# A four-layer convolution kernel: fourth neighbour and softplus sums to TensorE, a fifth scan product to VectorE

## The chip, the core and the metric

The kernel runs on one core of one Trainium2 chip. The metric is the device time of the whole kernel in microseconds. Work is spread over TensorE (PE; its weight loads are shown as PEld), VectorE (DVE), ScalarE (ACT) and GpSimd (POOL). SyncE (SP) issues most DMAs; POOL issues the indirect ones. Each engine takes its instructions in the order of the program and stops at an instruction whose inputs are not ready.

## The reference

Four layers are applied to an image batch x of shape (4, 128, 128, 128), each as x + layer(groupnorm(x)), all in f32.

- Layer 0 is a deformable 3x3 convolution. A small convolution gives, for each pixel and each of the 9 taps, an offset and a mask. Each tap is sampled bilinearly from four neighbours, each with its own weight:

```
corner(y0i, x0i, (1 - ly) * (1 - lx)) + corner(y0i, x0i + 1, (1 - ly) * lx)
  + corner(y0i + 1, x0i, ly * (1 - lx)) + corner(y0i + 1, x0i + 1, ly * lx)
```

  The sample, times its mask, is projected by a 128x128 matrix per tap and summed over the taps.
- Layer 1 is a dilated 5x7 convolution to 16 channels, followed by two small projections.
- Layer 2 norms the image, splits its channels, and passes one half through a selective scan in four directions with 16 states: h = h * exp(delta * A) + (delta * u) * B, and y = sum over the states of h * C. Here delta = softplus(dt), and B and C come from projections of u.
- Layer 3 is a 3x3 convolution with a term that subtracts neighbouring sums.

## The kernel before

**Two strands.** The scan of layer 2 is the main strand. It visits 4 images x 4 directions x 32 blocks of 512 positions, 512 blocks in all. Everything else is the side strand: generators that issue a few instructions each time they are pulled. `together` issues one scan slot (16 a block), then pulls the side until its share of progress matches. While image b is scanned, the side finishes image b-1 (after the scan, then layer 3) and prepares image b+1 (layer 0, layer 1, and the part of layer 2 ahead of the scan). So layer 0 runs once alone, for the first image, and three times beside the scan. `keep_order` fixes each engine's order as written. `loads` sets `beside["busy"]` to "POOL" while layer 0 runs beside the scan, and to "PE" for other side stages; the scan reads it to choose engines.

**Layer 0.** One sample is one tap of one block of 4 rows of 128 pixels: 32 x 9 = 288 samples an image. `weave` runs a software pipeline over samples with these steps:

1. `gather` (L416): four indirect DMAs by POOL fetch, for 128 pixels each, the four neighbours of 128 channels, into a tile g of [128, 4 rows, 4 neighbours, 128]. There are four such tiles.
2. `weigh_low` (L431), two steps later: ACT multiplies neighbours 1 and 2 in place by their per-pixel weights, and neighbour 0 into a PSUM bank, pw. There is one such bank.
3. `weigh` (L445): DVE adds neighbours 1 and 2 to pw in two additions (L450), then forms v = g3 * weight + pw for each row (L453). v has two tiles.
4. `turn` (L457), one step later: PE transposes the four 128x128 pieces of v into one PSUM bank, pst (L461).
5. `copy` (L463) moves pst to SBUF by ACT; `project` (L467) multiplies it by the tap's weights, accumulating over nine taps; `add` adds the residual at the ninth.

`order` (L504) fixes the order within a step: weigh_low of neighbour 1 and turn; then add, gather and weigh_low of neighbour 2; then weigh_low of neighbour 0; then copy and the work on the next strip's offsets; then weigh and project.

**The scan.** A block has four groups g of four states sets ng. For each group, DVE forms h = du * B (L972, 128x2048), with du in the one PSUM bank named dub, refilled by ACT in `inputs_up` (L876). For each ng, ACT makes the decay exp (L899) and DVE runs the scan (L1018). `outputs` (L935) multiplies half a group of h, 128x1024, by C: eight such products a block. PE sums them (L913, `sums`). `carry_on` saves the last column of h on ACT before the product overwrites h. While `beside["busy"]` is "POOL", the second half of every group is multiplied on DVE and the first half on POOL, so four of eight each; otherwise all are on POOL.

**prepare** (L822) makes delta two blocks ahead, one step a slot. PE multiplies u to pdt (in the dub bank). ACT takes e = |pdt|, delta = relu(pdt), then e = exp(-e), one_e = 1 + e, ln = log(one_e), one_e = one_e - 1. POOL then does delta = delta + (ln + (e - one_e)) in three additions (L858, L860, L862), one a slot, and du = delta * u (L864). The correction e - one_e restores what the rounding of 1 + e lost. The block's delta and du are stored to DRAM and read back spread over partitions.

Of the kernel before, what the change touches and what calls it, by code (L numbers as in the profile page):

```python
# [10 lines left out]
F32 = mybir.dt.float32  # L11
# [7 lines left out]
P = 128  # L19
# [4 lines left out]
N = R * W  # L24
# [7 lines left out]
NG = 4  # L32
# [79 lines left out]
def conv_preact_kernel(ctx: ExitStack, tc: tile.TileContext, a: dict, nb: int):  # L112
    nc = tc.nc
    x_in, out = a["x"], a["out"]

    const = ctx.enter_context(tc.tile_pool(name="const", bufs=1))
    small = ctx.enter_context(tc.tile_pool(name="small", bufs=2))
    dram = ctx.enter_context(tc.tile_pool(name="dram", bufs=2, space=DRAM))
    pss = ctx.enter_context(tc.tile_pool(name="scps", bufs=1, space=PSUM))
# [11 lines left out]
    beside = {}  # L131
# [19 lines left out]

    ident = const.tile([P, P], F32, name="ident")
    make_identity(nc, ident)
    started = len(tc.nc.cur_bb.bb.instructions)
    nc.scalar.preload_act_table_set(LOG_EXP)
    gmat = load(const, a["gmat"], [P, P], "gmat_sb")
# [23 lines left out]
    with ExitStack() as s:  # L180
# [3 lines left out]
        for k in range(NDIR):  # L184
            pw = bank(0, "pwd")
# [112 lines left out]
    def layer0(st):  # L298
# [5 lines left out]
        with ExitStack() as s:  # L304
# [30 lines left out]
            got = {}  # L335
# [108 lines left out]

            def weigh(n):  # L445
                i, k, j, q = where(n)
                wv, g = got["i", j][0], got.pop(("g", n))
                pw = got.pop(("w", n)).rearrange("p (r c) -> p r c", r=R)
                for c in (1, 2):
                    nc.vector.tensor_add(pw, pw, g[:, :, c, :])  # L450
                got["v", n] = v = gp.tile([P, R, P], F32, name="v", bufs=2)
                for r in range(R):
                    nc.vector.scalar_tensor_tensor(  # L453
                        v[:, r, :], g[:, r, 3, :], wv[:, r, q, k, 3:4], pw[:, r, :], ALU.mult, ALU.add
                    )

            def turn(n):  # L457
                v = got.pop(("v", n))
                got["t", n] = pst = bank(1, "pst")
                for r in range(R):  # L460
                    nc.tensor.transpose(pst[:, r * P : (r + 1) * P], v[:, r, :], ident)  # L461

            def copy(n):  # L463
                got["c", n] = smp = pp.tile([P, N], F32, name="smp")
# [322 lines left out]
    def scan(pull):  # L787
# [4 lines left out]
        seq = []  # L792
# [26 lines left out]
                    flush()  # L819
                blocks[t]["u"] = load(sp, blk(us[k % 2], i), [P, N], "u", bufs=2)  # L820

        def prepare(t):  # L822

            st, k, i, back = seq[t]
            c = blocks[t]
            if (st["b"], k) not in carries:
                carries[st["b"], k] = carry = small.tile([P, NST], F32, name="carry")
                nc.vector.memset(carry, 0.0)
            c["carry"] = carries[st["b"], k]
            u = c["u"]  # L830
            pdt = pss.tile([P, N], F32, name="pdt", tag="dub")
            nc.tensor.matmul(pdt, wd[:, k, :], u, start=True, stop=True)  # L832
            yield

# [12 lines left out]
            px = pss.tile([P, N], F32, name="pxbc", tag="dub")  # L847
            nc.tensor.matmul(px, xbc[:, k, :], u, start=True, stop=True)  # L848
            ln = sp.tile([P, N], F32, name="ln", bufs=1)
            nc.scalar.activation(ln, one_e, AF.Ln)  # L850
            yield
            nc.scalar.activation(one_e, one_e, AF.Identity, bias=minus)  # L852
            bc = sp.tile([2 * NST, N], F32, name="bc")
            nc.scalar.copy(bc, px[0 : 2 * NST])  # L854
            c["bc"] = bcd = dram.tile([2, NST, N], F32, name="bcd", bufs=4)
            store(bcd.rearrange("j s t -> (j s) t"), bc)
            yield
            nc.gpsimd.tensor_sub(e, e, one_e)  # L858
            yield
            nc.gpsimd.tensor_add(ln, ln, e)  # L860
            yield
            nc.gpsimd.tensor_add(delta, delta, ln)  # L862
            yield
            nc.gpsimd.tensor_mul(du, delta, u)  # L864
            c["steps"] = sd = dram.tile([P, 2 * N], F32, name="stepsd", bufs=4)
            store(sd, steps.rearrange("p j t -> p (j t)"))
# [93 lines left out]
        for t, (st, k, i, back) in enumerate(seq):  # L960
            c = blocks[t]
            carry = c["carry"]
            more = prepare(t + 2) if t + 2 < len(seq) else iter(())
            if t > 0:
                fetch(t + 3)
            for g in range(NG):
                then = (t, g + 1) if g + 1 < NG else (t + 1, 0)
# [7 lines left out]
                on_vector = beside.get("busy") == "POOL"  # L975
# [13 lines left out]
                for ng in range(NG):  # L989
                    n = g * NG + ng  # L990
                    if ng == 1:
                        decays(at + 1)
                        if before[0] >= 0 and not on_vector:
                            outputs(*before, 1)
                        if g > 1 and then[0] < len(seq):
                            inputs_up(*then)
                        if earlier[0] >= 0:
                            sums(*earlier, 1)
                    if ng == 2 and g == 1 and t > 0:
                        finish(t - 1)  # L1000
                    if n % NST and ng != 2:
                        next(more, None)
                    if ng == 2 and before[0] >= 0 and on_vector:
                        outputs(*before, 1, nc.vector)
                    if ng == 2:
                        carry_on(t, g, 0)
                        decays(at + 2)
                        next(more, None)
                        if g < 2:
                            inputs_up(*then)  # L1010
                    if ng == 3:
                        outputs(t, g, 0)
                        if before[0] >= 0:
                            sums(*before, 0)
                    o, f = h[:, ng, :], c["a", n]
                    if back:
                        o, f = o[:, ::-1], f[:, ::-1]
                    nc.vector.tensor_tensor_scan(o, f, o, carry[:, n : n + 1], ALU.mult, ALU.add)  # L1018
                    if ng == 3:
                        decays(at + 3)  # L1020
                    yield (t * NST + n + 1) / slots
            for _ in more:
                pass
        t = len(seq) - 1
# [408 lines left out]
```

## Time and profile before

| what | value |
|---|---|
| median of the timed runs | 22396.11 us (22355.13 to 22411.09, 3 runs) |
| the profiled execution: its own time, its span | 21942.39 us, 21940.6 us |
| busy over the span: PE, DVE, ACT, POOL | 74%, 86%, 75%, 78% |
| samples of layer 0 alone, beside the scan | 288, 864 |
| L424 gathers (POOL) | 4608, mean 988 ns |
| L450 additions (DVE) | 2304, mean 693 ns |
| L461 transposes (PE records) | 4608, mean 371 ns |
| L939 products: on POOL; on DVE | 3740, mean 2363 ns; 356, mean 1323 ns |
| L858, L860, L862 softplus additions (POOL) | 512 each, means 1272, 1274, 1291 ns |

Busy time is the union of an engine's instructions. For PE, one f32 matmul leaves two records; the ends of records are modelled, so distances between starts are the safer measure of cost. A row of a timeline merges equal instructions: start in us, length in us, engine, line, operation, output and inputs, shapes and count. A row of waits names who waited, for whom, the total us, the number of times and the longest. The span counts from the first instruction; the timed runs are of executions without a profile.

### The profile page before, as it was taken

How to read it: one execution, taken by the hardware profiler on the slowest of the kernel's cores; microseconds unless marked ns; L12 is line 12 of the kernel's file. 1: busy time of each engine (PE TensorE's matmuls, PEld its weight loads, DVE VectorE, ACT ScalarE, POOL GpSimd, SP SyncE). 2: the span in 40 equal slices, each digit the busy share in tenths (PEclk: the TensorE clock that was granted, in tenths of full speed). 3: DMA queues.
4: the chain of work that ended last, by engine and by line, in shares of the span. 5: the costliest groups of instructions: out<-in, count | busy, mean ns of one | idle time of the engine just before them, and what ended most of it. 6: DMA issues, size and time to landing. Idle time of an engine off the chain costs nothing. (4 is left out here: it accounts for less than half of the span.)

```text
span 21940.6 us, 177438 instructions
## 1 busy us (share of the span) xinstructions
PE 16289.2 (74%) x37000; PEld 6635.1 (30%) x37000; DVE 18903.6 (86%) x19821; ACT 16411.9 (75%) x37350; POOL 17213.1 (78%) x11496
## 2 busy tenths in 40 slices
PE   4557866666788878666688888766687878778788
PEld 1223322222333333222233333322233323233333
DVE  4554899999998899899998899998998899999994
ACT  5885868888688766788868776688877877666673
POOL 4773878877888888778788888787878889877884
PEclk6668988888999989888899999887898999999999
DMA  8775687777766968777776787777776677555674
GB/s 250 229 226 178 210 287 243 243 237 237 235 215 216 256 224 272 233 250 249 241 231 220 221 254 249 245 246 245 246 256 210 219 217 233 194 195 202 208 233 132
DMA packets 2578828, 5038.92 MB, mean 230 GB/s; under 512 B 1060736, under 2 KB 1333576, under 8 KB 2435408
## 3 DMA queue, kind: packets, MB, share of 16 engines
q1 hardware_dynamic: 2209104, 3819.31, 53.3%
q0 software_dynamic: 368640, 1208.25, 18.1%
q14 instruction: 782, 6.41, 0.1%
q8 instruction: 302, 4.95, 0.1%
HBM read 4082.03 MB, written 874.52 MB: 226 GB/s over the span
## 5 line engine op out<-in xcount | busy, mean ns | idle before, releaser
L1018 DVE TENSOR_TENSOR_SCAN h<-pa,carry,h 128x512 f32<-128x512 f32 x8192 | 9998.0, 1267 | 495.7 <-ACT pa L899 283.6
L913 PE MATMUL yacc<-h,gather_sb 128*128 128x512 f32 x15264 | 8338.4, 676 | 1770.5 <-POOL h L939 1170.3
L939 POOL TENSOR_TENSOR h<-h,cb 128x1024 f32<-128x1024 f32 x3740 | 8787.1, 2363 | 1093.0 <-ACT carry L933 1076.8
L424 POOL DMA_INDIRECT g<-table,idx x4608 | 4552.7, 988 | 1616.0 <-issue 1059.3
L899 ACT ACTIVATE pa<-spread,neg_a 128x512 f32<-128x512 f32 x8192 | 5488.2, 682 | 271.7 <-DVE h L1018 270.8
L972 DVE TENSOR_TENSOR h<-dub,bb 128x2048 f32<-128x2048 f32 x2048 | 4659.9, 2275 | 418.9 <-ACT dub L879 162.9
L913 PEld LDWEIGHTS yacc<-h,gather_sb 128*128 128x128 f32 x15264 | 3133.5, 216 | 6082.3 <-issue 3392.2
L461 PE MATMUL pst<-ident,v 128*128 128x128 f32 x4608 | 1194.5, 371 | 2578.5 <-DVE v L453 2236.1
L438 ACT ACTIVATE g<-g,wt 128x128 f32<-128x128 f32 x9216 | 2877.5, 389 | 301.5 <-DMA g<-table,idx 298.5
L933 ACT COPY carry<-h 128x2 f32<-128x2 f32 x4096 | 769.0, 188 | 3035.9 <-DVE h L1018 3031.8
L450 DVE TENSOR_TENSOR pw<-pw,g 128x512 f32<-128x512 f32 x2304 | 1597.7, 693 | 1073.6 <-ACT pw L438 1022.6
L438 ACT ACTIVATE pw<-g,wt 128x128 f32<-128x128 f32 x4608 | 1693.6, 368 | 291.2 <-DVE v L453 177.4
L461 PEld LDWEIGHTS pst<-ident,v 128*128 128x128 f32 x4608 | 718.5, 158 | 3938.6 <-issue 1901.5
L858 POOL TENSOR_TENSOR e<-e,one_e 128x512 f32<-128x512 f32 x512 | 651.2, 1272 | 1294.8 <-ACT one_e L852 1258.2
L471 PE MATMUL acc<-smp,w_sb 128*128 128x512 f32 x2304 | 1550.9, 762 | 56.1 <-DVE x L478 52.8
L879 ACT COPY dub<-spread 128x512 f32<-128x512 f32 x2048 | 1198.7, 585 | 391.2 <-DVE h L972 212.7
L453 DVE SCALAR_TENSOR_TENSOR v<-g,wt,pw 128x128 f32<-128x128 f32 x4608 | 1292.8, 342 | 113.7 <-DVE pw L450 2.8
L1238 PE MATMUL p<-xn,w_l_sb 128*128 128x508 f32 (+2 forms) x2304 | 1132.9, 610 | 1.8 <-ACT xn L1217 1.8
L848 PE MATMUL pxbc<-u,xbc_sb 128*128 128x512 f32 x1024 | 590.5, 660 | 394.4 <-DVE h L972 385.9
L721 PE MATMUL px<-win,convw_sb 128*128 128x508 f32 (+1 forms) x1536 | 786.8, 610 | 36.1 <-DMA win<-win 34.8
L941 POOL TENSOR_TENSOR h<-h 128x512 f32<-128x512 f32 x558 | 710.8, 1274 | 43.7
L832 PE MATMUL pdt<-u,wd 128*128 128x512 f32 x1024 | 562.4, 632 | 193.3 <-DVE h L972 127.4
(170 smaller groups left out, 16751.3 us busy)
## 6 DMA issues: line engine op xcount, KB each, us to landing
spread<-stepsd SPq DMA_DIRECT2D x2048, 512.0 KB, 4.3
bb<-bcd SPq DMA_DIRECT2D x512, 1024.0 KB, 8.0
cb<-bcd SPq DMA_DIRECT2D x512, 1024.0 KB, 9.1
stepsd<-steps SPq DMA_DIRECT2D x512, 512.0 KB, 3.5
table<-gt SPq DMA_DIRECT2D x512, 256.0 KB, 4.8
g<-table,idx POOLq DMA_INDIRECT x4608, 3.8
u<-urow SPq DMA_DIRECT2D x256, 256.0 KB, 3.5
yrow<-y SPq DMA_DIRECT2D x256, 256.0 KB, 9.3
```

The source lines that it names most:

```text
L424: nc.gpsimd.indirect_dma_start(out=g[:, r].rearrange("p q c -> p (q c)"), out_offset=None, in_=table, in_offset=bass.IndirectOffsetOnAxis( ...
L438: nc.scalar.activation(pw[:, r * P : (r + 1) * P] if c == 0 else g[:, r, c, :], g[:, r, c, :], AF.Copy, scale=wv[:, r, q, k, c : c + 1],)
L450: nc.vector.tensor_add(pw, pw, g[:, :, c, :])
L453: nc.vector.scalar_tensor_tensor(v[:, r, :], g[:, r, 3, :], wv[:, r, q, k, 3:4], pw[:, r, :], ALU.mult, ALU.add)
L461: nc.tensor.transpose(pst[:, r * P : (r + 1) * P], v[:, r, :], ident)
L471: nc.tensor.matmul(got["a", i], w0[:, k, :], got.pop(("c", n)), start=k == 0, stop=k == KK - 1)
L879: nc.scalar.copy(p, blocks[t]["p", g][:, 1, :])
L899: nc.scalar.activation(pa, blocks[t]["p", g][:, 0, :], AF.Exp, scale=neg_a[:, k, n : n + 1])
L913: nc.tensor.matmul(c["y"], gather[:, g, :], c["h", g][:, ng, :], start=g == 0 and ng == 0, stop=last and ng == parts[-1] and not second,)
L939: engine.tensor_mul(h, h, c["cb"][:, 2 * half : 2 * half + 2, :])
L972: nc.vector.tensor_tensor(h, c["pdu", g].unsqueeze(1).to_broadcast([P, NG, N]), c["bb"], ALU.mult)
L1018: nc.vector.tensor_tensor_scan(o, f, o, carry[:, n : n + 1], ALU.mult, ALU.add)
```

## The change

Three things change, the last two only while layer 0 runs beside the scan.

- `weigh` adds neighbour 1 alone. The addition of neighbour 2 moves to PE: for each of the four rows, `turn` now issues two matmuls with the identity as moving operand into the same piece of pst, one of g's neighbour 2 and one of v, accumulated. They are ordinary f32 matmuls where a transpose was. The tile g is thus read last by PE in `turn`, not by DVE in `weigh`. This holds for all 1152 samples.
- `prepare` with `on_pe` replaces POOL's three softplus additions by four accumulating matmuls, e, -one_e, ln and delta, with the identity or a negated identity `less` as weights, into the bank dub; ACT copies the sum to delta a slot later. The step product du moves one slot later. To keep the bank's users in order, `inputs_up` of groups 2 and 3 moves from slot ng = 1 to ng = 2.
- The first half of the last group, too, is multiplied on DVE: five of eight products.

```diff
             def weigh(n):
                 i, k, j, q = where(n)
-                wv, g = got["i", j][0], got.pop(("g", n))
+                wv, g = got["i", j][0], got["g", n]
                 pw = got.pop(("w", n)).rearrange("p (r c) -> p r c", r=R)
-                for c in (1, 2):
-                    nc.vector.tensor_add(pw, pw, g[:, :, c, :])
+                nc.vector.tensor_add(pw, pw, g[:, :, 1, :])
...
             def turn(n):
-                v = got.pop(("v", n))
+
+                v, g = got.pop(("v", n)), got.pop(("g", n))
                 got["t", n] = pst = bank(1, "pst")
                 for r in range(R):
-                    nc.tensor.transpose(pst[:, r * P : (r + 1) * P], v[:, r, :], ident)
+                    dst = pst[:, r * P : (r + 1) * P]
+                    nc.tensor.matmul(dst, g[:, r, 2, :], ident, start=True, stop=False)
+                    nc.tensor.matmul(dst, v[:, r, :], ident, start=False, stop=True)
...
+            if on_pe:
+                yield
+                yield
+                pd = pss.tile([P, N], F32, name="psum", tag="dub")
+                for n, (t, sign) in enumerate(((e, ident), (one_e, less), (ln, ident), (delta, ident))):
+                    nc.tensor.matmul(pd, sign, t, start=n == 0, stop=n == 3)
+                yield
+                nc.scalar.copy(delta, pd)
+                yield
+            else:
+                nc.gpsimd.tensor_sub(e, e, one_e)
+                yield
+                nc.gpsimd.tensor_add(ln, ln, e)
+                yield
+                nc.gpsimd.tensor_add(delta, delta, ln)
+                yield
             nc.gpsimd.tensor_mul(du, delta, u)
...
-            more = prepare(t + 2) if t + 2 < len(seq) else iter(())
+            on_pe = beside.get("busy") == "POOL"
+            more = prepare(t + 2, on_pe) if t + 2 < len(seq) else iter(())
...
-                        if g > 1 and then[0] < len(seq):
+                        if g > 1 and then[0] < len(seq) and not on_pe:
                             inputs_up(*then)
...
-                        if g < 2:
+                        if (g < 2 or on_pe) and then[0] < len(seq):
                             inputs_up(*then)
                     if ng == 3:
-                        outputs(t, g, 0)
+                        outputs(t, g, 0, nc.vector if on_vector and g == NG - 1 else nc.gpsimd)
```

More of the change, by code (lines that the diff above doesn't have):

```diff
@@ L153, in conv_preact_kernel @@
     make_identity(nc, ident)
+    less = const.tile([P, P], F32, name="less")
+    nc.vector.tensor_scalar_mul(less, ident, -1.0)
     started = len(tc.nc.cur_bb.bb.instructions)
@@ L820, in fetch, with prepare @@
                 blocks[t]["u"] = load(sp, blk(us[k % 2], i), [P, N], "u", bufs=2)
-        def prepare(t):
+        def prepare(t, on_pe=False):
             st, k, i, back = seq[t]
@@ L857, in prepare @@
             yield
[L858 to L863, printed above, removed]
+            if on_pe:
[14 more added lines that the diff above has]
+                yield
             nc.gpsimd.tensor_mul(du, delta, u)
```

## The prediction

> **What bounds the kernel now.** I began with the busy shares by stretch of time, taken for the four stretches in which the deformable layer runs: once alone, then three times beside the scan. Columns: stretch and its length, then for each engine busy us and instructions, then the granted PE clock, DMA share and GB/s.
>
> ```profile
> 217.00:1665.00 1448.00, 837.37 (x2252) 315.83 (x2252) 828.07 (x2015) 1246.23 (x3754) 1091.82 (x1152) 0.66 0.76 226
> 3245.00:5330.00 2085.00, 1360.58 (x3440) 555.55 (x3438) 1925.04 (x2811) 1803.08 (x4930) 1658.89 (x1416) 0.83 0.74 241
> 8885.00:10840.00 1955.00, 1285.87 (x3286) 535.04 (x3287) 1760.32 (x2700) 1719.27 (x4762) 1556.34 (x1375) 0.80 0.76 245
> 14125.00:16060.00 1935.00, 1264.73 (x3242) 524.75 (x3242) 1740.73 (x2676) 1707.45 (x4736) 1549.83 (x1370) 0.80 0.76 246
> ```
>
> The engine columns are PE, PEld, DVE, ACT, POOL. Beside the scan (5975 us in all, 864 of the layer's 1152 samples) DVE looks busiest with 5426 us (91%), ACT has 5229 (88%), POOL 4765 (80%), PE 3911 (65%). The share of POOL misleads, as the timeline shows:
>
> ```profile
> 1005.58 0.95 POOL L424 DMA_INDIRECT g<-table,idx  x1 [0.30 <-issue]
> 1006.83 0.94 POOL L424 DMA_INDIRECT g<-table,idx  x1 [0.30 <-issue]
> 1008.08 0.94 POOL L424 DMA_INDIRECT g<-table,idx  x1 [0.30 <-issue]
> ```
>
> Gathers follow each other at 1.25 us, of which 0.30 counts as idle that nothing releases. A sample's four gathers hold POOL for 5.0 us. Alone, 288 samples x 5.03 is the whole 1448 us: POOL is full there. In the stretch from 8885 (27.9 blocks of the scan), POOL holds 1152 x 1.25 = 1440, 111 products x 2.37 = 263, softplus and step products 28 x 5.4 = 151: 1854 of the 1910 us from first to last gather, 97%. So POOL and DVE both lead, with ACT close behind. The waits of the stretch from 8840 say how DVE and ACT are tied:
>
> ```profile
> DVE pw L450 <- ACT pw L438: 134.2, 96, 5.1
> ACT pw L438 <- DVE v L453: 66.7, 64, 2.8
> ```
>
> The weighed sum has one PSUM bank; ACT refills it only when DVE has read it. ACT's waits in the three stretches sum to 655 us: DVE accounts for about 437 (scan 235, weighed sum 177, carry 26), landings of gathers for 110, PE for most of the rest.
>
> **PE's price list.** Ends are modelled, so I use starts.
>
> ```profile
> 9617.71 0.60 PE L461 MATMUL pst<-ident,v 128*128 128x128 f32 x4
> 9618.24 1.06 PE L367 MATMUL po<-xs,ow_sb 128*32 128x508 f32 x8
> ...
> 1018.03 1.16 PE L461 MATMUL pst<-ident,v 128*128 128x128 f32 x4 [1.45 <-DVE v L453]
> 1018.98 1.91 PE L471 MATMUL acc<-smp,w_sb 128*128 128x512 f32 x2
> ...
> 21806.35 0.50 PE L1238 MATMUL p<-xn,edge 128*128 128x4 f32 x4
> 21806.72 7.93 PE L1238 MATMUL p<-xn,w_l_sb 128*128 128x512 f32 x18
> 21814.48 0.50 PE L1238 MATMUL p<-xn,edge 128*128 128x4 f32 x4
> ```
>
> Four transposes take 0.53 us at the fast clock (0.13 each) and 0.95 at the slow one (0.24). A 512-wide f32 record takes 7.76/18 = 0.43 fast; a 4-wide one 0.37/4 = 0.09, mostly its weight load.
>
> **What the Trainium skill says.** "FP8 and Floating Point Precision", TensorE Precision Notes: true f32 is four passes. The trace agrees in kind: an f32 matmul leaves two records (15264 of L913 for 7632 calls), a transpose one. "Perfetto Trace Analysis", Transposes: a standard matmul does work that a transpose skips; the change goes that way. "TensorE: Matmul & The Clock Gate", Part 1: PE is slow after an idle window of about 3.4 us and doubles its clock after as long a busy one. The trace agrees: transposes after short gaps run at 0.13, those after long gaps at 0.24 to 0.27, and the granted clock is 0.66 alone and 0.80 to 0.83 beside the scan, 0.94 and more where PE is dense. "SBUF — State Buffer", SBUF: two separate sides: DVE and GpSimd share a port pair as a lock. The trace agrees: the gather at 9611.64 took 1.86 us while DVE's product L939 ran from 9611.47; the mean gather is 993 ns from 9200 to 10700, 948 alone.
>
> **The change part by part,** for the three stretches (864 samples; 1402 scans there = 87.7 blocks).
> - DVE loses one of two additions a sample: two of them take 1.53 us start to start, so 0.72 x 864 = -622. It gains a product a block, 1.2 x 87.7 = +105. Net -517, to 4909.
> - POOL loses three additions (3 x 1.28) and a product (2.37): 6.2 x 87.7 = -545. The extra DVE product lengthens gathers: 45 ns x 902 gathers over 85 DVE products is 0.5 us each, +44. Net -500. Both engines are near full, so these cuts are on the path until the next engine binds.
> - ACT gains the copy of the sum: like L879, 0.51 us start to start, +45, to 5274. This is the new floor: at most 5975 - 5274 = 700 us could go.
> - PE: a sample's 4 transposes become 8 f32 matmuls of 128 columns, 16 records instead of 4. No row has that shape in a stream. Bounds at the fast clock: 0.09 (4-wide) to 0.30 (load 0.19 plus streaming 0.43/4, unoverlapped); I take 0.13, since four transposes show weights cycling at that rate and 0.11 of streaming fits beneath. So +12 x 0.13 = 1.6 us a sample fast, double slow. The sum of softplus is 8 records x 0.43 = 3.4 us a block fast, 6.9 slow. Together 1348 + 300 = +1650 fast.
> - Is PE full then? At fast prices the stretch 9200 to 10700 (225 samples) holds 680 x 0.43 (L913) + 452 x 0.43 (L471) + 900 x 0.13 + about 95 for the rest = 700 us, while PE shows 66% of 1500: a ratio of 1.4 for slow clock and pipeline ends. Beside the scan that is 2750 fast-priced us; 4400 after, 76% of 5780. More density means fewer idle windows, so I expect the ratio to fall to 1.15 to 1.25, and the clock to rise to about 0.9.
> - New waits. ACT's copy of a sample starts 2.0 to 5.9 us after the transposes do (9617.71 to 9619.67, 9643.08 to 9649.00); 16 records need 2.1 fast, 4.3 slow: some 0.1 us a sample, 85. Behind that copy in ACT's queue stand the next weighings and decays, for which DVE's scans wait. The four-term sum is issued one slot before its copy (a slot is 68/16 = 4.2 us) behind a pair of yacc sums (1.7 us): 5.1 us are needed, so ACT waits 1 to 2 us a block, about 130; now it waits 0.6 for pdt. POOL's step product stands behind this copy.
> - The gathered tile is released by PE instead of DVE, 2 to 4 us later. Four tiles give four periods, 26 us, for a round of gather 5, landing 4, ACT 4, DVE 2, PE 2 to 4: hidden; without that cover POOL would lose those 2 to 4 us a sample. dub is refilled a slot later, with two scans left, 8 us against a copy of 0.5: hidden by them. The fifth DVE product stands behind ACT's carry copy of one slot earlier; DVE's new idle (12 us a block) hides it. The constant `less` is 1 instruction.
> - Sum beside the scan: DVE's share of ACT's waits, 437, should fall by two thirds (-290) and unnamed small gaps by some 30, as DVE is a tenth lighter and POOL delivers sooner; the new PE waits give back about 215, of which half is stalled time that would be waited anyway, +105, and the new copy costs +45. That leaves -170 to -240; I take -210.
> - Alone (1448 us): POOL stays full, so DVE's cut is worth nothing. The slow PE needs 16 x 0.26 + 1.9 = 6.1 us a sample against a period of 5.03, the fast 3.0; saturated, it leaves the slow clock. I take +20, between 0 and +150.
>
> The sum is -190 on the execution profiled, 21942, hence 21752. The timed runs have a median of 22396, 454 longer with no profile to say where; I carry the difference over: 22396 - 190 = 22206.
>
> **Rivals.**
> 1. POOL was the only true bound, and ACT closes up to 96% busy: 5274/0.96 = 5494, -480 beside the scan; I allow -420 in all: 21980. For: 97% of POOL. Against: DVE's and ACT's mutual waits, and PE in the loop.
> 2. The relief is hidden: ACT waits for PE where it waited for DVE. PE waits at the full 215 plus 150 of queueing behind late v eat it: 22396, within 60. For: PE is in order, and pst already waits 542 us for v in the stretch from 8840, with everything queued behind it. Against: those waits fall where PE has nothing else.
> 3. Slower: PE becomes the bound. Place: the samples' 16 records. If the ratio stays at 1.4, PE needs 4400 x 1.4 = 6160 us, and with 3% of gaps 6350: +375; alone about +130: 22900. It decides from a ratio of 5975/4400 = 1.36, or from a record of 0.26 at the fast clock. For: today's 1.4. Against: saturation itself raises the clock.
>
> **How the numbers follow.** Mine 0.53, rival 1 0.16, rival 2 0.17, rival 3 0.14. A measurement of this kernel tells 0.3% (67 us) from nothing. Faster: most of mine (0.49) and rival 1: 0.65. Same: 0.04 of mine and 0.10 of rival 2: 0.14. Slower: rival 3 and 0.07 of rival 2: 0.21. Likeliest alone: 22080 to 22340. The range reaches down over most of rival 1 and up over rival 2 and the milder end of 3: 21930 to 22560.
>
> **What would show it.** Right: the stretches shrink to about 2005, 1890 and 1870 us; ACT at 91% or more; DVE near 85%; PE clock about 0.9; pst records 0.13 to 0.15 apart; waits of ACT on pst and on the sum below 250 us together. Wrong: PE busy above 90% with the clock still near 0.8 (rival 3); ACT's waits on pst or the sum above 350 us (rival 2); the alone stretch above 1500 us.

## The result and the profile after

The changed kernel takes 22,259.4 us, median of four runs (22,249.4 to 22,269.9), against 22,391.8 us before, measured beside it: a ratio of 0.9943 with an interval of 0.9926 to 0.9960, 132 us faster. The forecast was 22,206 within 21,930 to 22,560, with faster as the likeliest case. Most of the gain came from the stage for which the forecast had none, so that the nearness of the total is luck; the sections below show how.

One fact has to stand ahead of the numbers, because they can't be read without it. The kernels of one batch run on one chip, and the batches fell on chips of two kinds. On the **first kind** (one batch here, kernel before 21,911 us) the layer alone takes 1441 to 1443 us from its first gather to its last in the four versions profiled there; the profile of the kernel before that the forecast was read from, 21,942 us, has 1442. On the **second kind** (the result, and three more batches, kernel before 22,368 to 22,400 us) the kernel before takes 1843 us for it. The four batches of the experiments ran on four chips, once each, so that a lasting property of a chip and a passing one can't be told apart. So the forecast was read on one kind and measured on the other. For a comparison on one kind, the kernel before was profiled again on the second (e1_before). Here are two of its stretches, the layer alone and the second of the three beside the scan (the middle stretch), and then those of the changed kernel, in the columns of the forecast (stretch, length, then busy us of PE, PEld, DVE, ACT, POOL with instructions, granted clock, DMA share, GB/s).

```profile
218.00:2063.00 1845.00, 840.41 (x2240) 318.29 (x2240) 821.86 (x2004) 1225.04 (x3731) 1090.55 (x1152) 0.63 0.60 177
9272.00:11208.00 1936.00, 1256.74 (x3222) 521.66 (x3222) 1730.35 (x2657) 1694.54 (x4705) 1540.10 (x1367) 0.80 0.76 244
```

```profile
219.00:1975.00 1756.00, 1168.53 (x5660) 846.16 (x5661) 626.57 (x1721) 1229.91 (x3734) 1092.72 (x1152) 0.80 0.64 187
9157.00:11089.00 1932.00, 1564.17 (x6850) 958.45 (x6850) 1542.72 (x2397) 1699.10 (x4723) 1379.71 (x1260) 0.92 0.76 245
```

The reader should see two things. The work moved as planned: in the middle stretch DVE went from 1730 to 1543 us and POOL from 1540 to 1380, while PE went from 1257 to 1564 and its clock from 0.80 to 0.92. And yet that stretch has hardly become shorter, 1936 to 1932; the gain is in the first one, where the layer is alone, 1845 to 1756.

Where the relief beside the scan went is seen in the waits of the changed kernel's middle stretch, from 9157 to 11089 (engine, line, what it waited for: us in all, times, longest; here and in the later views of waits rows are picked out, and those of PE left out). "remote" is what the profile writes where it can't match the signal that ended the wait with an instruction that had just ended.

```profile
DVE pw L451 <- ACT pw L440: 277.1, 105, 6.3
POOL g L426 <- ACT smp L469: 128.0, 55, 3.4
ACT smp L469 <- remote: 67.8, 33, 4.4
ACT steps L869 <- PE psum L867: 25.3, 11, 5.2
ACT smp L469 <- PE acc L475: 18.4, 9, 3.8
ACT smp L469 <- PE pst L465: 15.6, 20, 2.1
ACT pa L913 <- DVE h L1033: 6.8, 10, 1.5
```

The waits of ACT for DVE, which led before (the same view of e1_before, from 9272 to 11208, has these two), are nearly gone, 4.0 and 6.8 us now:

```profile
ACT pw L438 <- DVE v L453: 65.2, 59, 2.8
ACT pa L899 <- DVE h L1018: 46.6, 48, 4.5
```

Their place is taken by ACT's copy of the sampled block (smp) and by its copy of the softplus sum (steps), both waiting for PE's results. POOL, free of additions, stands still instead until that smp copy lets PE and the gathered tiles move on.

PE's own rows are better than priced. In the timeline of the changed kernel, at the slow clock and at the fast one:

```profile
1011.63 0.63 PE L464 MATMUL pst<-ident,g 128*128 128x128 f32 x2
1012.06 0.63 PE L465 MATMUL pst<-ident,v 128*128 128x128 f32 x2
...
1016.27 0.39 PE L465 MATMUL pst<-ident,v 128*128 128x128 f32 x2
1016.49 0.39 PE L464 MATMUL pst<-ident,g 128*128 128x128 f32 x2
1016.72 0.39 PE L465 MATMUL pst<-ident,v 128*128 128x128 f32 x2
```

Two records are 0.43 us apart slow and 0.22 fast: 0.11 a record at the fast clock where I took 0.13.

### The profile page after: what moved, and what is told of

The parts are those of the page before. It is cut to its first block, busy times and chain, and to the rows that moved or that the text cites. A ratio compares the mean times of both kernels' runs of the same rounds, so it can differ in the third digit from the quotient of the medians.

```text
span 22249.8 us, 205910 instructions
## 1 busy us (share of the span) xinstructions
PE 17602.6 (79%) x51536; PEld 8526.4 (38%) x51536; DVE 18184.5 (82%) x18759; ACT 16428.7 (74%) x37439; POOL 16627.8 (75%) x11140
## 5 line engine op out<-in xcount | busy, mean ns | idle before, releaser
L953 POOL TENSOR_TENSOR h<-h,cb 128x1024 f32<-128x1024 f32 x3651 | 8576.3, 2363 | 1163.3 <-ACT carry L947 1125.0
L927 PE MATMUL yacc<-h,gather_sb 128*128 128x512 f32 x15264 | 7976.5, 650 | 1732.0 <-POOL h L953 1151.0
L927 PEld LDWEIGHTS yacc<-h,gather_sb 128*128 128x128 f32 x15264 | 3000.6, 207 | 5883.9 <-issue 3231.9
L464 PE MATMUL pst<-ident,g 128*128 128x128 f32 x9216 | 2133.4, 318 | 1350.8 <-ACT smp L469 1140.9
L464 PEld LDWEIGHTS pst<-ident,g 128*128 128x128 f32 x9216 | 1685.2, 224 | 2195.4 <-ACT smp L469 1666.1
L451 DVE TENSOR_TENSOR pw<-pw,g 128x512 f32<-128x512 f32 x1152 | 797.0, 692 | 1988.0 <-ACT pw L440 1716.1
L465 PE MATMUL pst<-ident,v 128*128 128x128 f32 x9216 | 2125.4, 318 | 320.4 <-DVE v L454 192.8
L465 PEld LDWEIGHTS pst<-ident,v 128*128 128x128 f32 x9216 | 1672.8, 226 | 415.9 <-DVE v L454 249.1
L475 PE MATMUL acc<-smp,w_sb 128*128 128x512 f32 x2304 | 1286.7, 642 | 13.6 <-issue 6.7
L469 ACT COPY smp<-pst 128x512 f32<-128x512 f32 x1152 | 668.2, 580 | 788.7 <-remote 612.1
```

Of the source, the lines that this page charges most:

```text
L464: nc.tensor.matmul(dst, g[:, r, 2, :], ident, start=True, stop=False)
L465: nc.tensor.matmul(dst, v[:, r, :], ident, start=False, stop=True)
L927: nc.tensor.matmul(c["y"], gather[:, g, :], c["h", g][:, ng, :], start=g == 0 and ng == 0, stop=last and ng == parts[-1] and not second,)
```

## The experiments

The table gives, for each profiled execution, the layer alone and beside the scan (three stretches together), from the first gather to the last, and beside it the median of the timed runs with its ratio to the kernel before on the same chip.

| kernel | kind | alone us | beside us | median us | ratio (95%) |
|---|---|---|---|---|---|
| before, as forecast from | looks like first | 1442 | 5882 | | |
| before, e1 | second | 1843 | 5930 | 22,396 | 1.0002 (0.9993 to 1.0010) |
| the change | second | 1754 | 5890 | 22,259 | 0.9943 (0.9926 to 0.9960) |
| the change, e9 | second | 1727 | 5877 | 22,206 | 0.9924 (0.9907 to 0.9940) |
| e2 neighbour only | second | 1759 | 5924 | 22,270 | 0.9941 (0.9924 to 0.9957) |
| e3 no neighbour | second | 1874 | 6228 | 22,720 | 1.0146 (1.0129 to 1.0163) |
| e11 no neighbour | second | 1873 | 6172 | 22,655 | 1.0125 (1.0108 to 1.0141) |
| e4 alone as before | second | 1871 | 5884 | 22,367 | 0.9987 (0.9980 to 0.9993) |
| e10 no softplus, g first | second | 1788 | 6008 | 22,386 | 1.0007 (1.0000 to 1.0014) |
| e12 five tiles, g first | second | 1806 | 6541 | 22,927 | 1.0234 (1.0217 to 1.0251) |
| e5 five tiles | first | 1443 | 5696 | 21,738 | 0.9921 (0.9904 to 0.9937) |
| e6 g first | first | 1441 | 5651 | 21,695 | 0.9903 (0.9887 to 0.9920) |
| e7 no softplus | first | 1442 | 5666 | 21,697 | 0.9905 (0.9888 to 0.9921) |
| e8 no fifth product | first | 1442 | 5708 | 21,752 | 0.9930 (0.9914 to 0.9947) |

The scan outside the stretches takes 13,672 to 13,712 us in the executions on either kind, the time before the scan without the layer alone 568 to 574, so what differs lies in the two columns. The stage alone is the same code in e1, e3, e4 and e11, and takes 1843, 1874, 1871 and 1873 us: one profiled execution is good to some 30 us there, and e1's was the fastest of its twelve runs (22,356 against a median of 22,396).

**e1_before: the kernel before, unchanged.**

> The kernel before, unchanged, for a second profile of it. The first profile covered 21942 us where the timed runs had 22391, and the changed kernel shows no such distance (22250 and 22259), so the two profiles can't be compared stage by stage until the 449 us are placed. Theory 1 (the first profile met an unusual execution): this one shows about 22390, and the excess over the first profile lies in one stage. If it lies in the deformable layer alone (1442 us from first to last gather in the first profile), that stage should now read about 1890. Theory 2 (profiling itself shortens this kernel): about 21942 again, with the alone stage at 1442.

It ran in 22,396 us. Its stages beside the first profile: alone 1843 against 1442 (+401), beside 5930 against 5882 (+49). Nearly all of the 454 us that the forecast carried over as a constant thus lies in one stage, as theory 1 asked, and it is the stage in which the forecast said POOL is full.

**e2_neighbour: the kernel before with PE's fourth neighbour only.**

```diff
-                for c in (1, 2):
-                    nc.vector.tensor_add(pw, pw, g[:, :, c, :])
+                nc.vector.tensor_add(pw, pw, g[:, :, 1, :])
...
-                    nc.tensor.transpose(pst[:, r * P : (r + 1) * P], v[:, r, :], ident)
+                    nc.tensor.matmul(dst, g[:, r, 2, :], ident, start=True, stop=False)
+                    nc.tensor.matmul(dst, v[:, r, :], ident, start=False, stop=True)
```

> The kernel before with one part of the change: the fourth neighbour is added by PE, in all 1152 samples; softplus's sums and the scan products stay on POOL as before. My prediction's terms: DVE 622 us lighter beside the scan, POOL as full as before, so no more than -60 beside the scan if POOL binds, and about -100 if DVE does. Rival (the alone stage loses by the wait of ACT's copy on PE): from first to last gather the alone stage takes about 1750 us as in the changed kernel, +300 against the first profile of before, and the total is 22650 or more if before's timed runs had a fast alone stage, 22350 if they had a slow one.

It gives the whole gain of the change on that kind, 0.9941 against 0.9943, and gives it in the layer alone: 1843 to 1759, with 5930 to 5924 beside the scan, where up to 60 or about 100 us less were expected. Beside the scan softplus's additions and the fifth product are still on POOL. The edit does two things to the stage alone: DVE loses an addition, and PE gets denser (its granted clock there rises from 0.63 to 0.81). No run gives PE the records and leaves DVE its addition, so which of the two shortens the stage isn't separated.

**e3_softplus_product, and the same kernel on another chip as e11_no_neighbour: the change without its neighbour part.**

```diff
-                nc.vector.tensor_add(pw, pw, g[:, :, 1, :])
+                for c in (1, 2):
+                    nc.vector.tensor_add(pw, pw, g[:, :, c, :])
...
-                    nc.tensor.matmul(dst, g[:, r, 2, :], ident, start=True, stop=False)
-                    nc.tensor.matmul(dst, v[:, r, :], ident, start=False, stop=True)
+                    nc.tensor.transpose(pst[:, r * P : (r + 1) * P], v[:, r, :], ident)
```

> The changed kernel without the fourth neighbour: PE only sums softplus, and DVE takes five of eight products; weigh and transposes are as before. Prediction's terms: POOL 500 us lighter, DVE 105 us heavier, ACT 45 heavier, so with DVE at 5530 of 5975 busy beside the scan there is little to win: -80 to +40 (22310 to 22430), alone stage as in the kernel before. Rival (POOL was the only bound): -250 or more beside the scan, 22140.

> The whole change without its neighbour part: DVE adds both neighbours and PE transposes v; softplus's sum on PE and the fifth product on DVE stay. Theory (DVE is over its budget with the fifth product, whatever the chip: 5341 us of work and 105 more in 5880): slower than before by 150 to 300 us on either chip, all of it beside the scan. Rival (the loss of 298 us beside the scan measured earlier came from the long waits of that chip alone): on a chip where the layer alone takes 1442 us, within 60 us of before.

Slower by 1.46% and 1.25%, beside the scan +298 and +242 over e1_before (e11 is from another chip of the second kind), where e3 was expected within -80 to +40 and e11, after it, at +150 to +300. The waits of e3's middle stretch, from 9389 to 11444, show both ends pulling:

```profile
DVE pw L452 <- ACT pw L440: 216.0, 97, 8.9
POOL g L426 <- ACT pw L440: 98.1, 61, 5.5
ACT smp L467 <- remote: 57.3, 15, 11.4
ACT pw L440 <- DVE v L455: 49.6, 42, 3.0
POOL steps L876 <- ACT steps L867: 47.0, 18, 4.0
ACT steps L867 <- PE psum L865: 42.2, 10, 5.3
```

ACT still waits for DVE, and now for PE's sum too; POOL's relief turns into standing still. So the two parts that unload POOL, one of which loads DVE, lose time together when DVE isn't unloaded (which of them costs it isn't separated), and the neighbour part, added to them, is worth 295 us beside the scan (6172 to 5877 on the same chip), though it is worth 6 by itself. The forecast's sum of independent terms has no room for such a thing. Both runs fell on the second kind, so that e11's second question, what this kernel does on the first, stays open.

**e4_beside_only: the change, but the layer alone keeps the two additions and the transposes.**

```diff
+    def layer0(st, alone=False):
...
+                for c in (1, 2) if alone else (1,):
+                    nc.vector.tensor_add(pw, pw, g[:, :, c, :])
...
+                    if alone:
+                        nc.tensor.transpose(dst, v[:, r, :], ident)
+                        continue
```

> The changed kernel, but the 288 samples of the deformable layer that runs alone keep the second addition on DVE and the transposes; the 864 beside the scan have the change. If the change costs time alone (312 us by the two first profiles) and its gain lies beside the scan, this is faster than the changed kernel by that cost: about 21950. If before's timed runs had as slow an alone stage as the changed kernel, this stage depends on something else, and the total is within 60 us of 22259, or above it.

The stage alone is back at 1871, the stretches beside the scan stay at 5884, and the gain falls from 132 to 32 us. The edit of the first stage is what the measured gain mostly consists of. Its 22,367 us lie above 22,259, as the second case of the expectation asked.

**e5_tiles: the change with five gathered tiles instead of four** (room for it from a single x1 and a tile shared by two short-lived offsets).

```diff
-            gp = s.enter_context(tc.tile_pool(name="l0g", bufs=4))
+            gp = s.enter_context(tc.tile_pool(name="l0g", bufs=5))
...
-                x1 = pp.tile([P, N], F32, name="x1")
+                x1 = pp.tile([P, N], F32, name="x1", bufs=1)
```

> The changed kernel with five gathered tiles g instead of four (paid for by one x1 tile less and one shared tile in the offsets' work). In the changed kernel POOL's gathers wait some 500 us beside the scan on ACT's copy, PE's transposes and ACT's weighing, which stand for the late release of g by PE. Theory 1 (that release is on the path, so my cover of 26 us a round was wrong): these waits fall under 200 us and beside the scan 5890 us become 5750 or less, total 22120 or less; alone 1754 becomes 1600 or less. Theory 2 (POOL waits because ACT is the bound and ACT waits for PE): the waits move elsewhere, total within 40 us of 22259.

**e6_g_first: PE takes the four products of g ahead of the four of v,** so that half its work of a sample doesn't wait for v.

```diff
-                    nc.tensor.matmul(dst, g[:, r, 2, :], ident, start=True, stop=False)
-                    nc.tensor.matmul(dst, v[:, r, :], ident, start=False, stop=True)
+                    nc.tensor.matmul(pst[:, r * P : (r + 1) * P], g[:, r, 2, :], ident, start=r == 0, stop=False)
+                for r in range(R):
+                    nc.tensor.matmul(pst[:, r * P : (r + 1) * P], v[:, r, :], ident, start=False, stop=r == R - 1)
```

> The changed kernel with PE's eight matmuls of a sample in another order: the four of neighbour 2, which need no DVE result, first, then the four of v. After v is ready PE has 8 records left instead of 16: 1.0 us less at the fast clock, 2.1 at the slow one. Theory 1 (ACT's waits for pst, 268 us beside the scan and 309 of 1200 us alone, are PE's work after v): they halve, total 22000 to 22160. Theory 2 (v has long been ready, and pst waits for the one bank that ACT's copy frees): order within the bank is worth nothing, total within 40 us of 22259.

**e7_neighbour_product and e8_neighbour_softplus: the change without softplus's sum on PE, and without the fifth product on DVE.**

```diff
-            if on_pe:
...
-                for n, (t, sign) in enumerate(((e, ident), (one_e, less), (ln, ident), (delta, ident))):
-                    nc.tensor.matmul(pd, sign, t, start=n == 0, stop=n == 3)
...
+            nc.gpsimd.tensor_sub(e, e, one_e)
```

```diff
-                        outputs(t, g, 0, nc.vector if on_vector and g == NG - 1 else nc.gpsimd)
+                        outputs(t, g, 0)
```

> The kernel before with the fourth neighbour on PE and the fifth product on DVE; softplus's sums stay on POOL. Against the neighbour alone (22270, beside the scan 5924): POOL 166 us lighter net of lengthened gathers, DVE 105 heavier with slack of a fifth. If POOL is a bound beside the scan: -60 to -120, 22150 to 22210. If ACT's waits for PE are the bound: within 40 us of 22270. Against the full change it lacks the sum on PE, for which ACT waited 122 us, and the copy, 45 us; POOL has 337 us more.

> The changed kernel without the fifth product: neighbour and softplus on PE, four of eight products on DVE. Against the neighbour alone (22270): POOL 337 us lighter, ACT 45 us heavier and waiting 122 us for the sum. If the sum's wait costs what POOL gains: within 40 us of 22270. If the sum alone made the run without the neighbour slow (22720), it costs here too: 22350 or more. If POOL binds: 22150 or less.

These four went to one chip, and it was of the first kind, while the totals expected are those of the second; so none of the four expectations is decided. They show the other split: alone nothing (1441 to 1443 against 1442), beside the scan 174 to 230 us less than the first profile, which isn't known to be from the same chip; by the timed runs, on one chip, 159 to 216 us less in all. Here is e6 by stretch:

```profile
219.00:1661.00 1442.00, 1029.34 (x5678) 706.75 (x5678) 626.11 (x1723) 1245.12 (x3741) 1091.27 (x1152) 0.90 0.76 227
8801.00:10642.00 1841.00, 1530.40 (x6850) 940.72 (x6850) 1547.35 (x2397) 1698.51 (x4726) 1377.16 (x1260) 0.93 0.79 257
```

ACT is at 1699 of 1841, 92%, DVE at 84%. Its waits in that stretch:

```profile
POOL g L426 <- PE pst L465: 61.8, 99, 4.4
POOL g L426 <- ACT pw L440: 42.9, 61, 2.9
ACT steps L869 <- PE psum L867: 34.6, 13, 5.7
ACT pa L913 <- DVE h L1033: 18.5, 27, 1.5
ACT pw L440 <- DVE v L454: 16.3, 23, 2.1
```

No wait of the smp copy is among those above 7.7 us, and none is "remote". What the two halves of POOL's relief are worth is small: leaving softplus on POOL (e7) or the product on POOL (e8) gives 5666 and 5708, both near the two versions that have everything (5696 and 5651). All four have the neighbour part, and no run on this kind leaves it out or has it alone; that it carries the gain there is likely, not shown. e5 and e6 can't be set against the change itself, which no batch took to this kind.

**e9_after: the change again.**

> The whole change once more, unchanged. Theory (the chip decides where the gain falls): on a chip where the layer alone takes about 1442 us from first to last gather, the change leaves that stage as it is (within 5 us) and takes 170 to 230 us off the three stretches beside the scan, so about 21720 against 21911 (ratio 0.990 to 0.993), with ACT waiting for PE's sum of softplus and pst together about 200 us; on a chip where that stage takes about 1843 us, it gives again about 1754 alone and 5890 beside, 22260 in all (ratio 0.994). Rival (the layer's gain on the first chip was a matter of that one execution): alone 1843 or 1442 in both kernels, and beside the scan the same 5890 on either chip.

It came to a chip of the second kind and repeated the result: 1727 alone, 5877 beside, ratio 0.9924. The rival asked for no gain in the stage alone, 1843 us on such a chip, and fails: the same chip gives 1873 without the neighbour part (e11). What the theory says of the first kind wasn't measured.

**e10_both: e7 with e6's order.**

> The fourth neighbour on PE, its four products ahead of the four of v, and the fifth scan product on DVE; softplus's three additions stay on POOL. Theory (the softplus sum's wait and PE's late transposes each cost a little, POOL still has room for the additions): 40 to 70 us below the whole change on the same chip, some 21650 to 21690 where the layer alone takes 1442 us. Rival (with the additions on POOL its gathers bind, and the order of PE's products is worth nothing there): no better than neighbour and fifth product in the old order, 21700 there, or above.

Theory and rival both asked for 0.990 or so on the first kind; it ran on the second and came to 1.0007 there, 180 us behind the change on the same chip, of which 132 lie beside the scan (6008 against 5877) and 61 alone. The theory's 40 to 70 us below the change missed by more than 200. In the three stretches its smp copies wait 347 us for "remote", against 132 in e9, and POOL's first softplus addition waits 215 for ACT. Whether the order, or softplus left on POOL, did it isn't separated here.

**e12_tiles_g_first: the change with five tiles and e6's order.**

> The whole change with five tiles for the gathers (x1 single, off in pos_c's tile) and PE's four products of the fourth neighbour ahead of those of v. Theory (the gathered tile's later release by PE costs POOL time, a little where the layer alone takes 1442 us and more where it takes some 1800): below both single versions, 21660 to 21690 on the first kind of chip (POOL's waits for PE's pst and ACT's copy under 100 us beside the scan); on the second kind 60 to 150 below the whole change, 22050 to 22150. Rival (the long waits of the second kind are not cured by a further tile, because the copy itself comes late and everything behind it): 22180 to 22260 there; and on the first kind the two gains do not add, 21695 or above.

Both expectations failed, by 650 us and more. Two edits that stand in kernels with ratios of 0.992 and 0.990 on the first kind make 1.0234 together on the second. Of the versions with the neighbour part, the two that don't gain on the second kind, e10 and e12, are the two in which PE takes the products of g first. That makes the order the suspect, but each of them has another edit as well. The middle stretch of e12 has grown by 240 us over the change's while every engine has the same work:

```profile
9402.00:11574.00 2172.00, 1609.17 (x6850) 999.35 (x6850) 1544.65 (x2396) 1698.17 (x4723) 1367.20 (x1260) 0.87 0.68 218
```

What grew is one wait and what stands behind it, in the view of waits from 9402 to 11574:

```profile
DVE pw L451 <- ACT pw L440: 389.1, 135, 10.2
ACT smp L469 <- remote: 313.5, 62, 13.4
POOL h L953 <- ACT carry L947: 236.2, 49, 9.1
POOL steps L878 <- ACT steps L869: 128.7, 25, 7.9
```

The smp copy's "remote" waits went from 68 us in 33 to 314 us in 62; the carry copies and decays that stand behind it in ACT's queue are what POOL and the scan then wait for.

## Why the prediction was right or wrong

**The total was right in sign and within the range; its make-up on the measured chips was not.** Forecast: -210 beside the scan, +20 alone, -190 in all. The terms named for the stretches beside the scan add up to -170; the forecast took -210, the other 40 us without a term. Measured on the second kind, the change against e1_before by profile: -40 beside, -89 alone, +30 in the rest of the scan, -3 before the scan, -102 (the spans differ by 104, the medians by 132). The second execution, e9, against the same: -53, -116, +22, +1, -146. With 1872 us for the stage alone, as in e3, e4 and e11, the gain there is about 30 us greater, and the first sum comes to about the 132 of the timed runs. So two errors of opposite sign met, and that the totals came out at 22,259 and 22,206 is luck: the mechanism forecast gave 40 to 53 us of its 210, and the stage forecast at +20 gave most of the rest.

**The engines' terms held.** In the three stretches, e1_before to the change: DVE 5366 to 4820, -546 (forecast -517); POOL 4699 to 4163, -536 (-500); ACT 5165 to 5188, +23 (+45). PE's busy time rose by 941 to 4785. With the change's 1650 the forecast had 4400 fast-priced us, a ratio of 1.09; at 0.11 a record the new work is 12 x 864 x 0.11 + 300 = 1440, 2750 + 1440 = 4190, a ratio of 1.14. I had said 1.15 to 1.25, and a clock of 0.9: it is 0.92. The page "TensorE: Matmul & The Clock Gate", Part 1, of the Trainium skill was the reason to expect that denser work is faster work, and the trace agrees (clock 0.80 to 0.92 in the middle stretch). The Trainium skill's page "Perfetto Trace Analysis", Transposes, says that a matmul does what a transpose skips; true of PE (0.53 us for a sample's four transposes, about 1.8 for its sixteen records), which was not the one to save. Rival 3 (PE becomes the bound) fell on the ratio, which had to stay above 1.36. The lengthening of gathers beside a DVE product was about 10 us in the middle stretch (mean 994 to 1003 ns over 1152) and 1 to 2 in each of the others, 13 in all against 44.

**Beside the scan: "the new PE waits give back about 215, of which half".** This is the step that failed on the second kind: it was to leave 170 to 240 us of gain, and 40 to 53 are left. ACT's waits for DVE did fall, from 370 us (pa 200, pw 170) to 54 (37 and 17), -316 where I had -290. But its waits on PE's side came to about 378: smp copies on "remote" 156, on pst 44, on the acc and yacc sums ahead in PE's queue 66, softplus's copy 111; before, the smp copies' were 34 and softplus's copy didn't exist. That is relief hidden by waits for PE, as in rival 2: e4, in which the stage alone is as before, takes 22,367, inside that rival's 22,396 within 60. But its reason, queueing in PE behind a late v, covers at most the 222 us that have a name, about the 215 of the forecast; the 156 more are signals that come late (below), which no case of the forecast held. Nor was "the gathered tile is released by PE, hidden" true: POOL's gathers wait 320 us for smp copies and 95 for pst in the three stretches, and 175 for pst in e6 on the first kind. On the first kind the rest of the step looks right: in e6 DVE's share of ACT's waits fell from 398 (pa 222, pw 176) to 139 (96 and 43), the softplus copy waits 142 and the smp copies 4 for pst, and the four versions measured there gain 174 to 230 beside the scan, about the 210 forecast. By stretch it is 75, 70 and 86 us (e6) or 49, 51 and 74 (e8), from first to last gather, where I had 80, 65 and 65; the 2005, 1890 and 1870 of the forecast are of windows cut 14 to 45 us wider. That the change itself would do the same there is likely, not shown.

Two of the signs set for being wrong came up: the stretch alone is above 1500 us, and the waits on PE's side are above 350 if the late signals are counted (pst and the sum by name are 155). The first says nothing of the change, since the kernel before takes 1843 there; the second is the failed step.

**Alone: "POOL stays full, so DVE's cut is worth nothing".** On the first kind, true to within 2 us, for the four versions measured. On the second the premise is false: POOL is held up. In e1_before the stage, from 400 to 1600, has these waits:

```profile
DVE pw L450 <- ACT pw L438: 445.4, 121, 13.2
POOL g L424 <- ACT pw L438: 237.2, 51, 11.2
ACT pw L438 <- remote: 181.6, 34, 8.8
ACT smp L465 <- remote: 81.7, 13, 12.5
```

POOL's 1.25 us a gather holds 1440 us of 1843; most of the rest it stands behind ACT, which waits for signals that the profile can't place. With one addition fewer in the loop of DVE, ACT and PE, and PE at a higher clock, a sample takes 6.1 us (1754/288) instead of 6.4. e4 shows that this edit of this stage is what is gained.

**"I carry the difference over".** The one assumption that I did not price: that 454 us of unknown place add to both kernels alike. They sat in the very stage that I costed at nothing. The forecast should have held a case in which the missing 454 us are slack in the layer alone, where every cut counts.

**What stays open: why signals come late.** In the windows compared (400 to 1600 and 9300 to 10800) ACT and DVE have such waits in every kernel profiled on the second kind, and none in e5 to e8 on the first, nor in the first profile of the kernel before. The changed kernel's timeline, cut to PE's last row for a copy, POOL's gathers and two of the waiters, shows their form:

```profile
1004.92 0.39 PE L465 MATMUL pst<-ident,v 128*128 128x128 f32 x2
...
1006.02 0.95 POOL L426 DMA_INDIRECT g<-table,idx  x1 [0.30 <-issue]
1007.27 0.94 POOL L426 DMA_INDIRECT g<-table,idx  x1 [0.30 <-issue]
1009.98 0.59 ACT L469 COPY smp<-pst 128x512 f32<-128x512 f32 x1 [3.42 <-remote]
1010.02 0.69 DVE L482 TENSOR_TENSOR x<-acc,xres 128x512 f32<-128x512 f32 x1 [1.51 <-remote]
1010.64 0.95 POOL L426 DMA_INDIRECT g<-table,idx  x1 [2.42 <-ACT smp L469]
```

PE's last record for that copy ended, as modelled, at 1005.31; the copy starts at 1009.98, together with a DVE instruction that waits for another of PE's results, 1.8 us after POOL's last gather ended. That is no single case: of the 98 such waits over 1 us in the changed kernel from 400 to 1600, 97 end while POOL stands idle for over 0.8 us or within 0.1 us after, though POOL does so for 21% of the time, and the median distance to the end of the last gather is 1.79 us, with quartiles 1.75 and 1.91. In e2 it is 97 of 99, in e9 78 of 97, in e12 54 of 72, in e1_before 26 of 47, where the distance is spread out (quartiles 0.67 and 2.9).

The trace also keeps each update of a semaphore, the counter by which an instruction tells the others that it is done, and these records show that the signals themselves are late. In e6, from 400 to 1600, PE has 2163 updates for 2163 instructions that make one, none more than 0.04 us after such an instruction's end, and a gather's landing makes 16. In the changed kernel, in the same window, there are 1364 for 1780; 475 of them come more than 1 us after the last such instruction ended, up to 6.6 us; and a landing shows 4.9 updates where it had 16. All nine profiles of the second kind are like that beside gathers, and none of the five of the first; and from 6500 to 8500, where the scan runs without gathers, the counts agree in all of them (1035 for 1035 in the changed kernel), none later than 0.02 us. The transfers are not slower: a gather's packet takes 0.18 us on average in both kernels. Since in that window a quarter of PE's records and two thirds of DVE's are missing, or stand for several updates at once, who waited for whom is less sure on the second kind than on the first.

It looks as if on those chips signals are held back while gathers follow each other, and let through when POOL pauses; then a tile more, which lets POOL run on, should make the waits longer, and in e12 they are (4.7 us on average from 400 to 1600 against 3.2). But so they are in e10, which has four tiles (4.7). The timeline of e12:

```profile
1014.41 0.95 POOL L426 DMA_INDIRECT g<-table,idx  x1 [0.30 <-issue]
1015.67 0.94 POOL L426 DMA_INDIRECT g<-table,idx  x1 [0.30 <-issue]
1017.43 0.59 ACT L469 COPY smp<-pst 128x512 f32<-128x512 f32 x1 [7.57 <-remote]
1020.89 0.95 POOL L426 DMA_INDIRECT g<-table,idx  x1 [4.27 <-ACT pw L440]
```

But POOL must pause when ACT is late, since ACT's work gives back its tiles, so the coincidence alone proves no direction; e12 changed two things; and no run spaced the gathers out by themselves. What holds the signals back, and why chips differ in it, isn't settled.

## What to carry to other kernels

Before carrying a gap between a profile and the timed runs over to the new kernel, ask in which stage it could sit: a stage that is full in one execution may be slack in another, and then the same cut has a different worth. When two engines and a third hold each other in a loop, price the loop and not the engines: beside the scan, on the second kind, the parts that unload POOL cost 242 to 298 us without the neighbour part and gained 34 to 47 with it (e2 5924, the change 5877 to 5890, one profiled execution each). A version is chosen on the chips that it will run on: of the versions measured here, e6 and e7 are the quickest on the first kind (0.9903 and 0.9905), and the change itself (0.9924 and 0.9943) with the neighbour alone (0.9941) on the second; none but the kernel before was measured on both kinds.

## What the runs showed of the hardware

The same program takes 21,911 us on one chip and 22,368 to 22,400 on others, 2.1 to 2.2% apart, while the repeats on one chip stay within 0.4%; by the two profiles of the kernel before, 401 us of it is one stage in which indirect gathers follow each other without a break (1442 against 1843). On the slower chips, and only beside gathers, semaphore updates of PE come up to 6.6 us late in the changed kernel (up to 15 in e1_before), and engines stand idle for late signals: by the waits over 1 us, 3.2 us on average in the changed kernel's stage alone, 5.8 in e1_before's, up to 13 beside the scan in e12. In the changed kernel and e2 most of these waits (87 of 98, 86 of 99) end 1.7 to 2 us after the end of POOL's last gather; in e1_before one of 47 does. A 128-column f32 matmul with fresh weights costs 0.22 us at PE's fast clock (two records of 0.11) and 0.43 at the slow one. PE's granted clock in the stage alone rose on the second kind from 0.63 to 0.80 with sixteen records a sample instead of four; in e4, which has four there, it is 0.63.
